# Keys of a linear-attention block transposed by DMA, block steps reordered, and 27 expert tiles turned by TensorE

## The chip, the cores and the metric

The kernel runs on one core of a Trainium2 chip. Its engines are TensorE (PE in the profile, with its weight loads as PEld), VectorE (DVE), ScalarE (ACT), GpSimd (POOL) and SyncE (SP, which here issues DMAs); 16 DMA engines move data for all queues. The metric is the device time of one execution in microseconds, as the median of several runs.

## The reference

The input is x of 8 sequences x 1024 tokens x 256 values, all float32. It is normalised per token, and the result is x plus a linear attention plus a mixture of experts, both of the normalised x.

```python
xn = _layernorm(x)
q = elu(xn @ Wq.T) + 1          # 16 heads of 16
k = elu(xn @ Wk.T) + 1
v = xn @ Wv.T
kv_cumsum = cumsum(einsum('blhd,blhe->blhde', k, v), axis=1)
k_cumsum = cumsum(k, axis=1)
out = einsum('blhd,blhde->blhe', q, kv_cumsum)
out = out / clip(einsum('blhd,blhd->blh', q, k_cumsum), 1e-6)
attention = out @ Wo.T

top, which = top_k(xn @ Wr + br, 2)      # 8 experts
c = softmax(top), put at the two experts
moe = sum over e of c[e] * ((silu(xn @ W1[e]) * (xn @ W3[e])) @ W2[e])   # inner size 512
result = x + attention + moe
```

## The kernel before

**Blocks and tiles.** The 8192 tokens are 16 blocks of 512 (`NBLK`, `TB`), each of four chunks of 128; two blocks make a sequence. The expert work is cut into tiles of 128 (token, expert) pairs, gathered by token number: 25 tiles of the first four blocks (`N1`), and then 107 of all that is left (`NM` = 132 in all; three more run only if the counts need them). A first part, in a `tc.manual_schedule` context, normalises and transposes the first four blocks, computes their router logits, the first lists of tokens, and block 0's q, k and v.

**The main loop.** `for j in range(NM + 1)` makes one pass for each expert tile. For j from 1 to 11 a pass also normalises, turns and routes one more block of x (block 4 + j); these blocks are read into five buffers (`f_x`, tag "xb") by `load_x`, some on SP's queue ahead of the loop, the others on ScalarE's queue five blocks ahead. For j from 12 to 21 a pass also builds a piece of the second lists (`second_batch`, almost all of it on VectorE). Then `attend_upto` makes one or more steps of attention, and `ffn_step(j)` does the expert tile: it gathers tile j + 4 on GpSimd (`ffn_load`), asks for the weights of tile j + 2 on SP (`ffn_weights`), runs the gate and up matmuls of tile j (`ffn_hidden`, L1261, 32 matmuls into two `gu_ps` banks of the four-bank pool `ps_mm`), prepares the transposed input of tile j + 1, and runs the output matmuls of tile j - 1 (`ffn_out`, L1280). Results are added to DRAM by GpSimd (L1291).

**How a tile is transposed.** The matmuls need a tile with its features on the partitions. For j below `TURNED` = 8, `ffn_turn` does it: two TensorE transpositions (L1226) and a ScalarE copy (L1228). Later tiles go as two-byte halves: `ffn_halves` splits each float32 into its low and high 16 bits on VectorE (L1198), `ffn_turn_halves` issues one transposing DMA on SP between the tile's two weight loads (L1207), and `ffn_join` puts the halves together on ScalarE (L1216).

**Steps of a block.** `block_steps(t)` drives the generator `project(t)`, then `scores` and `weigh` for the four chunks; it yields nine times, and each stretch between yields is a step. Of `project`, the pieces were grouped so: step 0 both halves of q (L795; `elu1` on ScalarE and VectorE, `mask_q` on ScalarE) and the output projection (`attend`, L993) of the last block's last chunk; step 1 the keys `kn` (L811); step 2 eight TensorE transpositions of `kn` (L858), the copies to `kT` (L861) and on VectorE the running sum of keys and its product with q (L863 to L868); step 3 the values (L811, copies L828) and the denominators (`den`, L880), whose reciprocals go through DRAM and come back spread over partitions as `rden`. Step 4 asks for the next block's input and makes the first scores (L917, masked by L924 on VectorE, four banks of `ps_mm`). `attend_upto(n)` makes at most n steps in all, at least one a pass if any is due, and joins a step to the one before it in the same pass only if it is step 0, 4 or 8. From pass 22 on, 121 steps are spread over 106 passes.

**What sets the order.** In the `manual_schedule` context the written order holds on TensorE, VectorE, ScalarE and GpSimd. Elsewhere a planner of the language orders each engine's instructions by their place in the program, by when it expects their inputs, and by free buffers; only instructions under `in_order` (all DMAs on SP, the norm and the join on ScalarE) keep the order they are written in. So SP is one strict queue, and a DMA that waits there holds up all later ones.

Of the kernel before, what the change touches and what calls it, by code (L numbers as in the profile page):

```python
# [46 lines left out]
F32 = mybir.dt.float32  # L47
I32 = mybir.dt.int32
BF16 = mybir.dt.bfloat16
U16 = mybir.dt.uint16  # L50
AF = mybir.ActivationFunctionType
ALU = mybir.AluOpType
AX = mybir.AxisListType

P = 128
# [9 lines left out]
def tile_attention_moe(  # L65
# [14 lines left out]
    nc = tc.nc  # L80
    B, L, H = x.shape
    E, _, I = w1.shape
    KC = H // P
    IC = I // P
    TB = 512
    NCH = TB // P
    N = B * L
    NBLK = N // TB
    BLK_PER_SEQ = L // TB
# [4 lines left out]
    FB = 4  # L94
# [4 lines left out]
    NM = NF - NR  # L99
# [11 lines left out]
    two = ctx.enter_context(tc.tile_pool(name="two", bufs=2))  # L111
# [4 lines left out]
    ps_t = ctx.enter_context(tc.tile_pool(name="ps_t", bufs=2, space=bass.MemoryType.PSUM))  # L116
# [4 lines left out]
    f_x = ctx.enter_context(tc.tile_pool(name="f_x", bufs=5))  # L121
# [17 lines left out]
    in_order = tc.keep_in_program_order  # L139
# [7 lines left out]
    def load_x(t, queue):  # L147
        xbs[t] = f_x.tile([P, NCH, H], F32, tag="xb", name=f"xb{t}")
        in_order(queue.dma_start(out=xbs[t], in_=xf[t]))
# [15 lines left out]
    for t in range(FB, FB + 2):  # L165
        load_x(t, nc.sync)

    ident = const.tile([P, P], F32, name="ident")
# [5 lines left out]
        out=causal, in_=causal, pattern=[[1, P]], compare_op=ALU.is_ge,  # L174
# [5 lines left out]
        out=before, in_=before, pattern=[[1, P]], compare_op=ALU.is_ge,  # L180
        fill=0.0, base=-1, channel_multiplier=-1,
    )
    ones = const.tile([P, P], F32, name="ones")
# [5 lines left out]
        out=own, in_=own, pattern=[[-HD, HALF]], compare_op=ALU.is_ge,  # L189
# [583 lines left out]
    sums = [None]  # L773
# [10 lines left out]
    def begin(t):  # L784
        names = dict(
            qT=[KC, TB], qm=[KC, 2, TB], kn=[NCH, H], kT=[KC, TB], rden=[NCH, KC, P]
        )
        tiles = {n: one.tile([P, *d], F32, tag=n, name=n) for n, d in names.items()}
        blocks[t] = tiles["qT"], tiles["qm"], tiles["kT"], tiles["kn"], va, tiles["rden"]
# [27 lines left out]
    def project_k(t, c):  # L817
        kn = blocks[t][3]
        z = project_kv(t, c, 0)
        yield from elu1(  # L820
            kn[:, c : c + 2, :].rearrange("p c h -> p (c h)"), z.rearrange("p c h -> p (c h)")
        )

    def project_v(t, c):
# [6 lines left out]
            )  # L831
        yield

    def project(t):


        if t > 0:
            begin(t)
            for o in range(KC):
                for _ in project_q(t, o):  # L840
                    pass
                mask_q(t, o)
                yield
            for c in range(0, NCH, 2):
                for _ in project_k(t, c):
                    pass
                yield
        else:
            for _ in range(4):
                yield  # L850
        qT, qm, kT, kn, va, rden = blocks[t]
        upto_t = two.tile([P, KC], F32, tag="upto_t", name="upto_t")
        fresh = t % BLK_PER_SEQ == 0
        qks = []
        for o in range(KC):
            tp = ps_t.tile([P, TB], F32, tag="t", name="tp")
            for c in range(NCH):
                nc.tensor.transpose(  # L858
                    tp[:, bass.ts(c, P)], kn[:, c, bass.ts(o, P)], ident
                )  # L860
            nc.scalar.copy(kT[:, o, :], tp)  # L861
            ksum = two.tile([P, TB], F32, tag="ksum", name="ksum")
            nc.vector.tensor_tensor_scan(  # L863
                ksum, ones[:, 0:1].to_broadcast([P, TB]), kT[:, o, :],
                0.0 if fresh else sums[0][:, o : o + 1], ALU.mult, ALU.add,
            )
            nc.vector.tensor_copy(upto_t[:, o : o + 1], ksum[:, TB - 1 : TB])
            nc.vector.tensor_tensor(ksum, qT[:, o, :], ksum, ALU.mult)  # L868
            qks.append(ksum)
            yield  # L870
        for c in range(0, NCH, 2):
            if t > 0:
                for _ in project_v(t, c):
                    pass
            yield

        den = ps_y.tile([P, P], F32, tag="y", name="den")
        for o in range(KC):
            for c in range(NCH):
                nc.tensor.matmul(  # L880
                    den[32 * c : 32 * c + 32, :], lhsT=own_of[:, o, :],
                    rhs=qks[o][:, bass.ts(c, P)], start=(o == 0), stop=(o == KC - 1),
                    skip_group_check=True,
                )
        over = one.tile([P, P], F32, tag="over", name="over")
        nc.vector.tensor_scalar(over, den, EPS_DEN, None, ALU.max)
        nc.vector.reciprocal(over, over)

        through = den_d[t % 2]
        for c in range(NCH):  # L890
            in_order(
                nc.sync.dma_start(
                    out=through[HEADS * c : HEADS * (c + 1)],
                    in_=over[32 * c : 32 * c + HEADS, :].unsqueeze(1).to_broadcast([HEADS, HD, P]),
                )
            )
        in_order(
            nc.sync.dma_start(
                out=rden.rearrange("p c o l -> p (c o) l"),
                in_=through.rearrange("(x h) d l -> (h d) x l", h=HALF),  # L900
            )
        )
        yield
        del xnTs[t]
        sums[0] = upto_t
# [103 lines left out]
    def block_steps(t):  # L1009


        for i, _ in enumerate(project(t)):
            if i == 1 and behind:
                attend(*behind.pop())
            if i in (1, 3, 5, 8):
                yield
        if t + 1 < NBLK:
            fetch(t + 1)
        waiting = scores(t, 0)
        yield  # L1020
        done = None
        for c in range(NCH):
            coming = scores(t, c + 1) if c + 1 < NCH else None
            if done and c + 1 < NCH:
                attend(*done)
            oT = weigh(*waiting)
            if done and c + 1 == NCH:
                attend(*done)
            done = t, c, oT
            waiting = coming  # L1030
            if c + 1 < NCH or t + 1 < NBLK:
                yield
        behind.append(done)
        if t + 1 == NBLK:
            attend(*behind.pop())
            yield
# [97 lines left out]
    with tc.issue_after(last_store[0].ins):  # L1134
        for a in range(4):
            some = slice(a * E // 4, (a + 1) * E // 4)
            in_order(
                nc.sync.dma_start(
                    out=w2_sb.rearrange("p (c h) -> p c h", h=H)[
                        :, a * E * IC // 4 : (a + 1) * E * IC // 4, :  # L1140
                    ],
                    in_=w2[some].rearrange("e (c p) h -> p (e c) h", p=P),
                )
            )
        load_x(FB + 2, nc.sync)

        for t in range(FB):
            rows = slice(t * TB, (t + 1) * TB)
            in_order(nc.sync.dma_start(out=acc_d[rows, :], in_=x_rows[rows, :]))
        in_order(nc.sync.dma_start(out=wo_sb, in_=woT.rearrange("(k p) o -> p k o", p=P)))  # L1150
    table = nc.sync.dma_start(
        out=tab_d[0].rearrange("(p j i) w -> p j (i w)", j=2, i=FT),
        in_=tab.rearrange("p (j i) w -> p j (i w)", j=2)[:, :, 0 : FT * 3],
# [19 lines left out]
    def ffn_load(j):  # L1173
        table, _, num_i, src_i, _, _, i = of_tile(j)
        xg[j] = ffn4.tile([P, H], F32, tag="xg", name="xg")
        nc.gpsimd.indirect_dma_start(  # L1176
            out=xg[j], out_offset=None, in_=x_rows[:, :],
            in_offset=bass.IndirectOffsetOnAxis(ap=src_i[:, i : i + 1], axis=0),
        )
        entry[j] = ffn8.tile([P, 3], F32, tag="entry", name="entry")  # L1180
        nc.gpsimd.indirect_dma_start(  # L1181
            out=entry[j], out_offset=None, in_=table[:, :],
            in_offset=bass.IndirectOffsetOnAxis(ap=num_i[:, i : i + 1], axis=0),
        )
# [114 lines left out]
    def ffn_step(j, behind):  # L1299


        if j + 4 < NM:
            ffn_load(j + 4)
        if j + 2 < NM:
            ffn_weights(j + 2)
        if j < NM:
            ffn_hidden(j, j == NM - 1)
        if j + 1 < TURNED:
            ffn_turn(j + 1)
        elif j + 1 < NM:  # L1310
            ffn_join(j + 1)
        if j > 0 and j != NM - 1:
            ffn_out(j - 1)
        for _ in range(2):
            if stored[0] < j - behind:
                ffn_store(stored[0])
                stored[0] += 1


    TURNED = 8  # L1320
    for j in range(4):
        ffn_load(j)
    for j in range(2):
        ffn_weights(j)
    for i in range(3, 6):
        load_x(FB + i, nc.sync)
    ffn_norm(0)
    ffn_turn(0)
    LATE = 3
# [105 lines left out]
```

## Time and profile before

| | |
|---|---|
| median of 3 runs | 1288.55 us (1285.26 to 1289.98) |
| the profiled execution's own time | 1289.82 us |
| its span, first to last instruction | 1287.7 us |
| mean granted TensorE clock | 0.985 |
| TensorE busy | 1221.5 us |
| VectorE, ScalarE, GpSimd busy | 681.8, 558.6, 522.7 us |
| DMA engines, mean over 300 to 1260 us | 0.87 busy |

Rows of a group are to be read as: line, engine, operation, output<-input, shapes, count, then busy time in us and mean length of one in ns, then the idle time of the engine ahead of them and what ended it. A row of a timeline has start, length, line, engine, what, count, and in brackets a wait ahead of it with its releaser. Lengths of neighbouring matmuls overlap, so the distance from one start to the next tells what one costs in a stream. "SPq" and "ACTq" rows are DMA issues.

### The profile page before, as it was taken

To read this page: it belongs to the slowest core of one execution; us is meant where nothing else is said; L and a number is where in the kernel's file an instruction comes from. 1 tells how busy PE (TensorE), PEld (TensorE's weight loads), DVE (VectorE), ACT (ScalarE), POOL (GpSimd) and SP (SyncE) were. 2 spreads that over 40 slices of the span, in tenths; PEclk is the share of its full clock that TensorE was granted. 3 is DMA by queue.
4 is the path that set the end of the run, shared out by engine and by line. 5 is a ranking of instruction groups with operands and counts; after the bars stand their busy time and mean duration, and the time that the engine had idled before them with its cause. 6 is when DMAs were issued, how large, how long until landed. Compare 5 with 4: busy or idle time off the path is not lost. (4 is left out here: it accounts for less than half of the span.)

```text
span 1287.7 us, 30871 instructions
## 1 busy us (share of the span) xinstructions
PE 1221.5 (95%) x12064; PEld 1046.7 (81%) x12064; DVE 681.8 (53%) x1560; ACT 558.6 (43%) x1060; POOL 522.7 (41%) x460
## 2 busy tenths in 40 slices
PE   5789999899999999999999999999999999999995
PEld 3578786678888888888888888888888888888885
DVE  7867489764354454535453544445453536354541
ACT  4556465372442626262625344262626262444420
POOL 3634334214334444444342534443443534343522
PEclk9889999899999999999999999999999999999998
DMA  9898776659699898889796989989888979897983
GB/s 341 269 293 240 174 196 156 198 136 246 132 277 211 169 222 189 198 188 225 158 234 145 210 182 212 197 173 226 177 206 173 231 168 220 172 211 164 213 186 62
DMA packets 230929, 256.79 MB, mean 199 GB/s; under 512 B 83554, under 2 KB 154850, under 8 KB 230498
## 3 DMA queue, kind: packets, MB, share of 16 engines
q1 hardware_dynamic: 187394, 200.58, 55.6%
q0 software_dynamic: 38064, 43.22, 24.8%
q10 hardware_dynamic: 5328, 11.01, 2.4%
q8 instruction: 99, 1.62, 0.6%
q14 instruction: 44, 0.36, 0.1%
HBM read 196.30 MB, written 52.67 MB: 193 GB/s over the span
## 5 line engine op out<-in xcount | busy, mean ns | idle before, releaser
L1261 PE MATMUL gu_ps<-xgT,w 128*128 128x128 f32 x4224 | 514.0, 279 | 19.5 <-DVE s_sb L924 8.3
L1261 PEld LDWEIGHTS gu_ps<-xgT,w 128*128 128x128 f32 x4224 | 493.6, 194 | 37.3 <-DVE s_sb L924 12.2
L1291 POOL DMA_INDIRECT out_dram<-y,dst_i x107 | 175.8, 1643 | 296.3 <-issue 67.2
L1280 PE MATMUL y_ps<-w_sb,hT 128*128 x1056 | 251.2, 380 | 1.5 <-DVE hT L1272 0.9
L1176 POOL DMA_INDIRECT xg<-in_x_dram,src_i x132 | 130.6, 990 | 244.4 <-DVE half L1198 183.7
L1269 ACT ACTIVATE hT<-gu_ps 128x512 f32<-128x512 f32 x132 | 78.8, 597 | 321.2 <-PE gu_ps L1261 320.9
L1280 PEld LDWEIGHTS y_ps<-w_sb,hT 128*128 128x128 f32 x1056 | 190.4, 190 | 23.6 <-DVE hT L1272 1.0
L924 DVE TENSOR_TENSOR s_sb<-s_ps,causal 128x512 f32<-128x512 f32 x256 | 162.8, 683 | 70.5 <-PE o_ps L951 41.3
L1198 DVE COPY half<-xg 128x512 uint16<-128x512 uint16 x124 | 54.3, 438 | 149.1 <-ACT xg L1188 148.9
L1272 DVE TENSOR_TENSOR hT<-gu_ps,hT 128x512 f32<-128x512 f32 x132 | 90.5, 685 | 65.9 <-PE gu_ps L1261 42.2
L1181 POOL DMA_INDIRECT entry<-tab_d,of_i x107 | 106.1, 992 | 36.6 <-issue 32.0
L1287 DVE TENSOR_SCALAR y<-y_ps,entry 128x256 f32<-128x256 f32 x132 | 63.6, 482 | 107.3 <-PE y_ps L1280 107.0
L998 ACT COPY at<-a_ps 128x256 f32<-128x256 f32 x64 | 23.6, 370 | 168.0 <-PE a_ps L993 168.0
L1216 ACT COPY xgT<-halfT 128x512 uint16<-128x512 uint16 x124 | 94.1, 759 | 5.4 <-DMA halfT<-half 5.4
L917 PE MATMUL s_ps<-qm,kT 32*128 32x256 f32 x1024 | 86.5, 406 | 2.0 <-DVE hT L1272 1.9
L1291 POOL DMA_INDIRECT acc_d<-y,src_i x25 | 41.7, 1669 | 99.7 <-DVE y L1287 46.8
L1188 ACT ACTIVATE xg<-xg,entry 128x256 f32<-128x256 f32 x132 | 78.4, 594 | 3.9 <-DMA xg<-in_x_dram,src_i 3.2
L917 PEld LDWEIGHTS s_ps<-qm,kT 32*128 32x128 f32 x1024 | 51.6, 184 | 26.3 <-issue 19.4
L993 PE MATMUL a_ps<-wo_sb,oT 128*128 128x256 f32 x256 | 71.6, 403 | 1.0 <-DVE oT L968 1.0
L951 PE MATMUL o_ps<-s_sb,va 128*32 128x128 f32 x2048 | 69.5, 274 | 0.0
L993 PEld LDWEIGHTS a_ps<-wo_sb,oT 128*128 128x128 f32 x256 | 45.8, 194 | 23.1 <-issue 14.4
L795 PE MATMUL zq<-xnT,wq_sb 128*128 128x512 f32 x128 | 60.2, 610 | 0.0
(213 smaller groups left out, 1316.3 us busy)
## 6 DMA issues: line engine op xcount, KB each, us to landing
w<-in_w_dram SPq DMA_DIRECT2D x264, 512.0 KB
den_d<-over SPq DMA_DIRECT2D x64, 128.0 KB
rden<-den_d SPq DMA_DIRECT2D x16, 512.0 KB
xnT_d<-xnT ACTq DMA_DIRECT2D x15, 512.0 KB
xnT<-xnT_d SPq DMA_DIRECT2D x15, 512.0 KB
out_dram<-in_x_dram SPq DMA_DIRECT2D x12, 512.0 KB
out_dram<-at POOLq DMA_DIRECT2D x12, 512.0 KB
xb<-in_x_dram SPq DMA_DIRECT2D x10, 512.0 KB
```

Source lines behind the costliest of these rows:

```text
L917: nc.tensor.matmul(s_ps[r][:, hh].rearrange("p a l -> p (a l)"), lhsT=kT[rows, hh, span], rhs=qm[rows, hh, :, span], start=True, stop=True,)
L924: nc.vector.tensor_tensor(sm, s_ps[r].rearrange("p k a l -> p (k a) l"), causal_b, ALU.mult)
L993: nc.tensor.matmul(a_ps, lhsT=oT[:, hh, :], rhs=wo_sb[:, hh, :], start=(hh == 0), stop=(hh == 1),)
L1176: nc.gpsimd.indirect_dma_start(out=xg[j], out_offset=None, in_=x_rows[:, :], in_offset=bass.IndirectOffsetOnAxis(ap=src_i[:, i : i + 1], a ...
L1181: nc.gpsimd.indirect_dma_start(out=entry[j], out_offset=None, in_=table[:, :], in_offset=bass.IndirectOffsetOnAxis(ap=num_i[:, i : i + 1], ...
L1188: nc.scalar.activation(xg[j], xg[j], AF.Identity, bias=entry[j][:, 1:2], scale=entry[j][:, 2:3])
L1216: nc.scalar.copy(xgT[j].bitcast(U16).rearrange("p k (l b) -> p b k l", b=2), halves.pop(j).rearrange("p (b k) l -> p b k l", b=2),)
L1261: done = nc.tensor.matmul(ps[:, i, :], lhsT=w13[:, k, bass.ts(i, P)], rhs=xgT[j][:, k, :], start=(k == 0), stop=(k == KC - 1),)
L1269: silu = nc.scalar.activation(hT, gu[0], AF.Silu)
L1272: nc.vector.tensor_tensor(hT, gu[1], hT, ALU.mult)
L1280: done = nc.tensor.matmul(y_ps, lhsT=hT[:, i, :], rhs=w2_sb[:, bass.ds(e * (IC * H) + i * H, H)], start=(i == 0), stop=(i == IC - 1),)
L1291: nc.gpsimd.indirect_dma_start(out=rows[:, :], out_offset=bass.IndirectOffsetOnAxis(ap=dst_i[:, i : i + 1], axis=0), in_=ys.pop(j), in_off ...
```

## The change

The keys of blocks 1 to 15 are no longer transposed by TensorE. In `project`, step 0 now makes the keys and splits them on VectorE into two planes of 16-bit halves (`planes`, in buffers of the pool that held x). Step 1 issues four transposing DMAs on SP and makes q. Step 2 makes the values, joins the transposed halves on ScalarE into `kT`, and runs the key sums. Step 3 has the denominators alone. The held-back `attend` follows the first piece. Block 0 keeps TensorE transpositions. x of blocks 7 and 8 is asked for on SP ahead of the store of the table, block 9's after the first weights. `TURNED` is 27, and until pass 22 a tile is gathered three passes ahead, then four as before.

```diff
+    def key_sums(t, o, upto_t, qks):
+        qT, kT = blocks[t][0], blocks[t][2]
+        ksum = two.tile([P, TB], F32, tag="ksum", name="ksum")
+        nc.vector.tensor_tensor_scan(
+            ksum, ones[:, 0:1].to_broadcast([P, TB]), kT[:, o, :],
+            0.0 if t % BLK_PER_SEQ == 0 else sums[0][:, o : o + 1], ALU.mult, ALU.add,
+        )
+        nc.vector.tensor_copy(upto_t[:, o : o + 1], ksum[:, TB - 1 : TB])
+        nc.vector.tensor_tensor(ksum, qT[:, o, :], ksum, ALU.mult)
+        qks.append(ksum)
+
+    def planes(name):
+        tile_ = f_x.tile([P, NCH, H], F32, tag="xb", name=name)
+        return tile_.rearrange("p c h -> p (c h)").bitcast(U16)
+
     def project(t):
+        upto_t = two.tile([P, KC], F32, tag="upto_t", name="upto_t")
+        qks = []
         if t > 0:
             begin(t)
+            kT, kn = blocks[t][2:4]
+            halves_k = planes("k_half").rearrange("p (c b h) -> p c b h", c=NCH, b=2)
+            for c in range(0, NCH, 2):
+                for _ in project_k(t, c):
+                    pass
+                nc.vector.tensor_copy(
+                    halves_k[:, c : c + 2],
+                    kn[:, c : c + 2].bitcast(U16).rearrange("p c (h b) -> p c b h", b=2),
+                )
+            yield
+            turned_k = planes("k_halfT").rearrange("p (b o l) -> p b o l", b=2, o=KC)
+            for c in range(NCH):
+                in_order(
+                    nc.sync.dma_start_transpose(
+                        out=turned_k.rearrange("p b o l -> p (b o) l")[:, :, bass.ts(c, P)],
+                        in_=halves_k[:, c].rearrange("p b h -> p (b h)"),
+                    )
+                )
             for o in range(KC):
                 for _ in project_q(t, o):
                     pass
                 mask_q(t, o)
-                yield
+            yield
             for c in range(0, NCH, 2):
-                for _ in project_k(t, c):
-                    pass
-                yield
...
                 for _ in project_v(t, c):
                     pass
+            for o in range(KC):
+                nc.scalar.copy(
+                    kT[:, o].bitcast(U16).rearrange("p (l b) -> p b l", b=2),
+                    turned_k[:, :, o],
+                )
+                key_sums(t, o, upto_t, qks)
             yield
...
         for i, _ in enumerate(project(t)):
-            if i == 1 and behind:
+            if i == 0 and behind:
                 attend(*behind.pop())
-            if i in (1, 3, 5, 8):
-                yield
+            yield
...
         in_order(nc.sync.dma_start(out=wo_sb, in_=woT.rearrange("(k p) o -> p k o", p=P)))
+        for t in range(FB + 3, FB + 5):
+            load_x(t, nc.sync)
...
-        if j + 4 < NM:
-            ffn_load(j + 4)
+        while loaded[0] < min(NM, j + (5 if j >= READ else 4)):
+            ffn_load(loaded[0])
+            loaded[0] += 1
...
-    TURNED = 8
-    for j in range(4):
+    TURNED = 27
+    for j in range(3):
         ffn_load(j)
+    loaded = [3]
     for j in range(2):
         ffn_weights(j)
-    for i in range(3, 6):
-        load_x(FB + i, nc.sync)
+    load_x(FB + 5, nc.sync)
```

Block 0's branch does what the old code did for every block (eight transpositions, copies, key sums), with the sums moved into `key_sums`.

More of the change, by code (lines that the diff above doesn't have):

```diff
@@ L842, in project @@
                 mask_q(t, o)
-                yield
+            yield
             for c in range(0, NCH, 2):
-                for _ in project_k(t, c):
-                    pass
-                yield
-        else:
-            for _ in range(4):
-                yield
[L851 to L872, printed above, removed]
                 for _ in project_v(t, c):
                     pass
-            yield
+            for o in range(KC):
[4 more added lines that the diff above has]
+                key_sums(t, o, upto_t, qks)
+            yield
+        else:
+            kT, kn = blocks[t][2:4]
+            yield
+            yield
+            for o in range(KC):
+                tp = ps_t.tile([P, TB], F32, tag="t", name="tp")
+                for c in range(NCH):
+                    nc.tensor.transpose(
+                        tp[:, bass.ts(c, P)], kn[:, c, bass.ts(o, P)], ident
+                    )
+                nc.scalar.copy(kT[:, o, :], tp)
+                key_sums(t, o, upto_t, qks)
+            yield
+        rden = blocks[t][5]
         den = ps_y.tile([P, P], F32, tag="y", name="den")
@@ L1012, in block_steps @@
         for i, _ in enumerate(project(t)):
-            if i == 1 and behind:
+            if i == 0 and behind:
                 attend(*behind.pop())
-            if i in (1, 3, 5, 8):
-                yield
+            yield
         if t + 1 < NBLK:
```

## The prediction, made before the changed kernel ran

> **What bounds the kernel now.** I read the page first: the busy times, then the span in 40 slices.
>
> ```profile
> PE 1221.5 (95%) x12064; PEld 1046.7 (81%) x12064; DVE 681.8 (53%) x1560; ACT 558.6 (43%) x1060; POOL 522.7 (41%) x460
> ...
> PE   5789999899999999999999999999999999999995
> ```
>
> TensorE is the bound from about the sixth slice on, and no other engine is near it. Over 300 to 1260 us it is busy 947 of 960 us, and its waits there come to 12.5 us, 5.3 of them (8 waits, 0.7 at most) for the mask multiplication L924. So whatever leaves TensorE in that stage is worth its full price, and work on the other engines costs nothing unless TensorE comes to wait for it. The timeline of TensorE in one block (start, length, line, what) shows the price list:
>
> ```profile
> 566.05 3.62 PE L811 MATMUL zkk<-wkv_sb,xnT 128*128 128x256 f32 x16
> 569.50 3.73 PE L1261 MATMUL gu_ps<-xgT,w 128*128 128x128 f32 x32
> 573.07 1.89 PE L1280 MATMUL y_ps<-w_sb,hT 128*128 x8
> 574.80 1.04 PE L858 MATMUL tp<-ident,kn 128*128 128x128 f32 x8
> 575.67 3.74 PE L1261 MATMUL gu_ps<-xgT,w 128*128 128x128 f32 x32
> 579.25 1.89 PE L1280 MATMUL y_ps<-w_sb,hT 128*128 x8
> 580.98 3.62 PE L811 MATMUL zkv<-wkv_sb,xnT 128*128 128x256 f32 x16
> 584.52 0.64 PE L880 MATMUL den<-ksum,own_of 128*32 128x128 f32 x16
> 585.10 1.36 PE L917 MATMUL s_ps<-qm,kT 32*128 32x256 f32 x16
> 587.11 3.84 PE L1261 MATMUL gu_ps<-xgT,w 128*128 128x128 f32 x32 [0.66 <-DVE s_sb L924]
> ```
>
> Each row starts where the last one's stream ends, so a row costs the distance to the next start. The eight transpositions of the keys cost 575.67 - 574.80 = 0.87 us, and one wait of 0.66 us stands after den and scores.
>
> Then the first 100 us, in windows (us, busy us of PE, PEld, DVE, ACT, POOL, clock, DMA share, GB/s):
>
> ```profile
> 36.00:40.00 4.00, 2.60 (x21) 1.81 (x25) 3.90 (x9) 3.94 (x12) 3.59 (x4) 1.00 0.55 203
> 40.00:44.00 4.00, 3.15 (x62) 2.27 (x61) 1.78 (x8) 1.64 (x5) 0.18 (x1) 1.00 0.31 84
> 44.00:48.00 4.00, 3.88 (x18) 2.19 (x16) 4.00 (x17) 3.98 (x8) 3.09 (x4) 1.00 1.04 347
> 48.00:52.00 4.00, 0.00 (x0) 0.00 (x0) 3.48 (x21) 0.80 (x3) 3.09 (x4) 0.82 1.04 352
> ```
>
> The DMA engines idle at 36 to 44 and are full from 44, while TensorE stands still at 48 to 52: ScalarE waits until 51.5 for the first gathered tile (issued 45.4), the first expert's input.
>
> **The change, part by part.**
>
> *Keys off TensorE.* Blocks 1 to 15 lose eight transpositions each: 15 x 0.87 = **-13.0 us**. Here a rule has to be weighed. The row has 273 ns for one:
>
> ```profile
> L858 PE MATMUL tp<-ident,kn 128*128 128x128 f32 x128 | 17.4, 273 | 0.0
> L1226 PE MATMUL xg_t<-ident,xg 128*128 128x128 f32 x16 | 3.5, 294 | 4.3 <-ACT xg L1188 4.3
> L1198 DVE COPY half<-xg 128x512 uint16<-128x512 uint16 x124 | 54.3, 438 | 149.1 <-ACT xg L1188 148.9
> L1216 ACT COPY xgT<-halfT 128x512 uint16<-128x512 uint16 x124 | 94.1, 759 | 5.4 <-DMA halfT<-half 5.4
> L861 ACT COPY kT<-tp 128x512 f32<-128x512 f32 x32 | 17.3, 587 | 9.2 <-PE tp L858 9.0
> ```
>
> The Trainium skill (TensorE: Matmul & The Clock Gate, Part 4, PE-mode transpose) puts one at about 275 ns in a kernel, mostly access latency. The row's length agrees, but in a stream these latencies overlap: 109 ns from start to start. By the page's figure this part would be -33 us and the next +10; I take the starts.
>
> *Tiles 8 to 26 turned by TensorE.* 19 tiles x 2 transpositions: at 118.02 such a pair stands in the stream and the next row starts at 118.24, so 19 x 0.22 = **+4.2 us** (+3.5 with the five tiles that fall into the stage where VectorE is the limit free, +5.6 at 294 ns each). ScalarE copies 0.37 us in place of 0.76, VectorE loses 19 copies of 0.43, SP 19 issues of 1.21 us. At 220 to 240 us VectorE is busy 19.15 of 20 us and TensorE only 14.94, with one wait of 4.2 us for a joined tile (xgT, L1216). Tiles of passes 12 to 21 are in this stretch: some eight copies, 3.5 us, go from VectorE, but the halves of blocks 1 and 2 bring 3.2 back. What is left is the shorter chain of a tile: between 0 and -4.2, taken as **-1**.
>
> *x read ahead.* 1 MB (two loads of 512 KB) moves from behind the first weights (SP, 44.2 us) to ahead of the table store, into the idle stretch. At 350 GB/s it takes 3.0 us out of the full stretch. Two waits can shrink: the first tile's at 48 to 52, and VectorE's 5.0 us at 75.8 to 80.8 for a later x load, after which TensorE waits 1.5 and 3.0 us (L917, L1261). The table is issued at 36.8 and first read at 43.8, so 3 us in front of it are covered; uncovered they would cost 3. Between +3 and -6, taken as **-3**, the bytes' own time once. Gathers are issued one tile later until pass 22, two passes ahead of use (15 us) against 6 us of landing: nothing.
>
> *What is added to a block, all beside TensorE.* VectorE: two copies of 128x1024 halves, between 0.7 (start to start of the 512 form, doubled) and 0.88 us each. In the keys' step they fit between the two kn results and hT, which waits for ScalarE's table load and SiLU until 7.6 us after the step begins anyway. Such copies run 512 elements in 0.43 us, and the skill (SBUF - State Buffer, the "DVE blocks DMA" trap) warns that a fast VectorE copy shuts GpSimd out while it writes descriptors. By the rule that is up to 30 x 0.88 = 26 us of GpSimd time; it is busy 41%, and its longest wait, 183.7 us for half (L1198), is for a buffer that is gathered two passes early. No TensorE wait, so 0. ScalarE: two joins of 128x1024 take the place of two kT copies (L861), 1.16 to 1.52 us against 0.59; step 2 then holds 4 va copies (1.3 us), joins (2.7), SiLU, join and norm of a tile (1.9): 5.9 of 9.2 us.
>
> SP: four transposing issues of 1.21 us (5 us), in order ahead of that pass's weights. They wait for the halves, done 7.5 us after the keys' step begins; behind them w1 of tile X+2 goes out at about 11.5 instead of 7.3 us, the tile's own transposition and w3 follow, and ScalarE and TensorE want those at 23 us and later. They land 3.3 us after issue (547.57 to 550.9), the last at 14.5 us; the joins' step begins at 18.4. **0**, with 4 us of cover for the joins. The DMA engines: the packet records show 512 packets of 256 B for each transposition, 24.5 ns each, 0.78 us of all 16 engines. 60 come and 19 go: +32 us over a span with 0.87 busy; no weight is waited for now.
>
> *Order of the steps.* Keys and q change places: both take 3.5 us of TensorE. But v now carries the key sums (scan, product: 3.7 us of VectorE), and den comes right after, where before the cheap transposition step lay a pass earlier. If ScalarE joins before it copies v, the sums end 5 us into the pass, before hT, and nothing is late. If after, joins end at 6.9 us, the sums at 9.4, hT at 10.0, y at 10.4: den waits 0.3, scores 0.2, the next gu_ps 1.45 instead of 0.66 us. Ten of the 15 blocks have den and scores in one pass. Between 0 and +13; the written order is not binding outside the first section and ScalarE is idle 3.5 us ahead of v (L828), so I take **+1.3**.
>
> Sum: -13.0 + 4.2 - 1 - 3 + 1.3 = **-11.5 us**. The profiled execution took 1289.8 us (span 1287.7 and 2.1 around it), 1.3 above the median of 1288.55. It would become 1278.3, the median **1277.0**.
>
> **Rivals.** (B) *Den and scores come late.* VectorE has the sums behind the joins in ten blocks: the upper value above, 13 instead of 1.3: 1288.7. For it: L924 is already the largest wait; against: the idle ScalarE. (C) *Slower: the joins wait for their transposition in ScalarE's strict order.* If the order places joins as soon as data is expected (pass of q) and four transpositions land later than that, SiLU, xgT and so gu_ps queue behind. At 2 us in each of 15 blocks: 1277.0 + 30 = 1307. It decides from 1.2 us a block (18 us turn -11.5 into +6.5). For it: the DMA engines show shares over 1.0 in many windows; against: 124 transpositions today cost ScalarE two waits, 5.4 us in all. (D) *The first 300 us give more:* both early waits (4.5 us) and the 4.2 us wait at 240 go, 5 more than taken: 1272.
>
> **How the numbers follow.** This case 0.50 (1272 to 1283 by the bounds of its terms), D 0.17, B 0.20, C 0.13. About 0.5%, 6.4 us, is what a measurement of this kernel can tell: faster is below 1282.1, slower above 1295. Faster: 0.46 + 0.17 + a tail of B, 0.64; same: 0.04 + 0.17 of B, 0.21; slower: C and 0.02 of B, 0.15. The range, 1268 to 1291, leaves out C and the end of D.
>
> **What would show it.** L858 at x8 only; xg_t (L1226) at x54 and 0.22 us a pair; the order keys, q, v, den on TensorE with no row of 0.87 us between; no wait of den L880 over 0.3 us and L924 still about 5 to 7 us over 300 to 1260 (B: 15 and more); ScalarE's waits for the transposed keys near zero (C: 30 and more); TensorE starting gu_ps before 53.3 us. The prediction is wrong if the stretch from tile 23 to the end isn't some 11 us shorter, whatever the first 300 us do.

## The result, and the profile after

The changed kernel takes 1377.78 us (median, 1372.89 to 1382.55) against 1288.78 for the kernel before, measured beside it: ratio 1.0684, 95% interval 1.0656 to 1.0711. It is 6.8% slower where -0.9% was forecast, and far outside the range of 1268 to 1291.

The profiled execution has a span of 1380.8 us at a granted clock of 0.958 (before: 1287.7 at 0.985). The page's first lines, as they were read before:

```profile
PE 1240.4 (90%) x11982; PEld 1056.2 (76%) x11982; DVE 702.9 (51%) x1571; ACT 603.9 (44%) x1086; POOL 519.7 (38%) x460
...
PE   5789998989699998989898999989898999979796
```

TensorE has 82 matmuls fewer and is nevertheless busy 19 us longer, and the slices from the ninth on are no longer solid nines. The chain of waits names the place; a row has the engine and line that waited, the releaser, the sum in us, how many times, the longest.

```profile
DVE ksum L838 <- ACT kT L885: 130.3, 27, 16.1
ACT kT L885 <- DMA k_halfT<-k_half: 122.0, 13, 13.0
...
PE zkv L811 <- DVE qT L765: 71.4, 13, 10.7
```

ScalarE's joins (L885) wait 122.0 us for the transposed keys, 13 times. VectorE's key sums wait for the joins. And TensorE's projection of the values waits 71.4 us, also 13 times, for half of q (`qT`). Before, it had no wait at all:

```profile
L811 PE MATMUL zkv<-wkv_sb,xnT 128*128 128x256 f32 x256 | 58.1, 379 | 0.0
```

What have the values to do with q? The tenth block, number 9 when counted from 0 as below, shows it. ScalarE from the end of the keys' pass:

```profile
814.91 0.60 ACT L1218 ACTIVATE xg<-xg,entry 128x256 f32<-128x256 f32 x1
824.86 1.33 ACT L885 COPY kT<-k_halfT 128x1024 uint16<-128x1024 uint16 x1 [9.35 <-DMA k_halfT<-k_half]
826.07 0.58 ACT L762 ACTIVATE neg<-zq 128x512 f32<-128x512 f32 x1
826.55 1.32 ACT L885 COPY kT<-k_halfT 128x1024 uint16<-128x1024 uint16 x1
827.88 1.28 ACT L763 ACT_TABLE_LOAD   x1
829.18 0.63 ACT L763 ACTIVATE neg<-neg 128x512 f32<-128x512 f32 x1
```

The first join stands *ahead* of q's activations (L762, L763) on ScalarE, though it is written a step behind them. It waits 9.35 us, and q waits behind it. TensorE in the same block:

```profile
806.75 3.62 PE L811 MATMUL zkk<-wkv_sb,xnT 128*128 128x256 f32 x16
...
816.36 3.60 PE L795 MATMUL zq<-xnT,wq_sb 128*128 128x512 f32 x8
819.80 3.73 PE L1291 MATMUL gu_ps<-xgT,w 128*128 128x128 f32 x32
823.37 1.89 PE L1310 MATMUL y_ps<-w_sb,hT 128*128 x8
830.59 5.21 PE L811 MATMUL zkv<-wkv_sb,xnT 128*128 128x256 f32 x16 [5.33 <-DVE qT L765]
836.07 3.84 PE L1291 MATMUL gu_ps<-xgT,w 128*128 128x128 f32 x32 [0.27 <-ACT xgT L1246]
```

q's two sums (`zq`) and the tile's two `gu_ps` hold all four banks of `ps_mm`. They are read out by q's activations, so the values can't start until 830.59: a wait of 5.33 us. And the row itself is 5.21 us long instead of 3.62. Windows over the last wait and the row (columns as in the prediction, the clock being the third number from the end):

```profile
824.00:830.50 6.50, 1.26 (x6) 0.76 (x4) 3.54 (x5) 5.59 (x7) 0.38 (x1) 0.98 0.88 278
830.50:836.00 5.50, 5.21 (x16) 4.04 (x16) 2.41 (x5) 5.46 (x8) 2.10 (x2) 0.71 0.08 7
```

After a standstill of 5.3 us the granted clock is 0.71; in block 6, after 4.6 us, it is 0.50. The Trainium skill (TensorE: Matmul & The Clock Gate, Part 1) has a rule for this: an idle window of about 3.4 us throttles the array to half its clock, and about 3.4 us of activity release it. From the page's figures one would estimate that a standstill costs 1.7 us more than its length. Measured over blocks 3 to 15, the sixteen matmuls of the values take 77.0 us in place of 13 x 3.62 = 47.1: 30.0 us, or 2.3 a block (0.1 to 3.1), which is more than that estimate. Nor is the edge sharp here: behind a standstill of 3.12 us (block 13) they take 3.72 us, behind one of 3.20 (block 4) 5.24.

The two sums, 71.4 + 30.0 = **101.4 us**, can be set against a ruler: the start of the output matmuls (`y_ps`) of tile 24, and of the last tile, 131, in each kernel. Blocks 3 to 15 lie between.

```
us                               to tile 24   24 to 131
before                              337.5       935.1
changed                             337.5      1030.1
changed, joins unfed                329.6       927.5
```

So up to tile 24 nothing was won or lost by the whole change, and behind it 1030.1 - 927.5 = 102.6 us hang on what the joins wait for. The last row is the first experiment, in which the joins read data that need no DMA ("unfed").

### The profile page after: what moved, and what is told of

Read it like the earlier page. It is cut to its first block, busy times and chain, and to the rows that moved or that the text cites. A ratio compares the mean times of both kernels' runs of the same rounds, so it can differ in the third digit from the quotient of the medians.

```text
span 1380.8 us, 30847 instructions
## 1 busy us (share of the span) xinstructions
PE 1240.4 (90%) x11982; PEld 1056.2 (76%) x11982; DVE 702.9 (51%) x1571; ACT 603.9 (44%) x1086; POOL 519.7 (38%) x460
## 5 line engine op out<-in xcount | busy, mean ns | idle before, releaser
L1321 POOL DMA_INDIRECT out_dram<-y,dst_i x107 | 172.4, 1611 | 306.4 <-DVE y L1317 176.5
L811 PE MATMUL zkv<-wkv_sb,xnT 128*128 128x256 f32 x256 | 90.3, 524 | 71.4 <-DVE qT L765 71.4
L811 PEld LDWEIGHTS zkv<-wkv_sb,xnT 128*128 128x128 f32 x256 | 67.8, 274 | 91.3 <-DVE qT L765 76.6
L1228 DVE COPY half<-xg 128x512 uint16<-128x512 uint16 x105 | 45.0, 429 | 131.3 <-ACT xg L1218 131.2
L885 ACT COPY kT<-k_halfT 128x1024 uint16<-128x1024 uint16 x30 | 39.6, 1329 | 122.0 <-DMA k_halfT<-k_half 122.0
L1246 ACT COPY xgT<-halfT 128x512 uint16<-128x512 uint16 x105 | 79.5, 757 | 0.2 <-DMA halfT<-half 0.2
L946 PEld LDWEIGHTS s_ps<-qm,kT 32*128 32x128 f32 x1024 | 50.1, 185 | 26.2 <-issue 20.6
```

The source lines that it names most:

```text
L811: nc.tensor.matmul(z[:, i, :], lhsT=xnTs[t][:, k, bass.ts(c + i, P)], rhs=wkv_sb[:, k, a, :], start=(k == 0), stop=(k == KC - 1),)
L946: nc.tensor.matmul(s_ps[r][:, hh].rearrange("p a l -> p (a l)"), lhsT=kT[rows, hh, span], rhs=qm[rows, hh, :, span], start=True, stop=True,)
L1246: nc.scalar.copy(xgT[j].bitcast(U16).rearrange("p k (l b) -> p b k l", b=2), halves.pop(j).rearrange("p (b k) l -> p b k l", b=2),)
L1321: nc.gpsimd.indirect_dma_start(out=rows[:, :], out_offset=bass.IndirectOffsetOnAxis(ap=dst_i[:, i : i + 1], axis=0), in_=ys.pop(j), in_off ...
```

## The experiments

**Theory W**, formed on this trace: the loss is one thing, the wait of two instructions that stand too early in ScalarE's strict order; the transpositions cost nothing by themselves. Against it stands **L**: the 60 transpositions load SP's queue and the DMA engines, and weights or tiles come late, with the waits as a symptom. And **O**: the new order of the steps is what costs. A third question is the second half of the change (x ahead, 27 tiles).

### Joins that wait for nothing

The joins read the halves as they are, not transposed; the transpositions are issued and nobody reads them. The output is that of other keys.

```diff
-                    kT[:, o].bitcast(U16).rearrange("p (l b) -> p b l", b=2),
-                    turned_k[:, :, o],
+                    kT[:, o].bitcast(U16).rearrange("p (c h b) -> p b c h", c=2, b=2),
+                    halves_k[:, 2 * o : 2 * o + 2].rearrange("p c b h -> p b c h"),
```

> The changed kernel, but the joins read the halves as they were before the transposition, from VectorE's own copy; so what lies in kT is not the transposed keys, and the outputs are those of other keys. The 60 transposing DMAs are still issued, unread. Only the wait of the joins for a DMA is taken away, at an early place on ScalarE. Theory W: 1275 to 1290 us, TensorE waits for qT under 5 us. Theory L: the DMAs run as before, 1360 to 1380 us. Theory O: 1350 to 1380 us.

Measured: 1270.83 us, ratio 0.9864 (0.9844 to 0.9884), 4 us below the range expected. All 60 transpositions are there, and the values' matmuls wait for nothing:

```profile
L811 PE MATMUL zkv<-wkv_sb,xnT 128*128 128x256 f32 x256 | 60.5, 387 | 0.0
```

L falls, and with it O, since the steps have the new order. Not only the wait is gone, though: the planner now puts the first join still earlier, 6.0 us behind the keys' step in block 9 where it was free for it at 8.8, so the key sums come early too.

```profile
758.80 1.35 ACT L885 COPY kT<-k_half 128x1024 uint16<-128x1024 uint16 x1 [0.21 <-DVE k_half L863]
```

Two copies ahead of q therefore cost nothing by themselves; they cost when they stand there and wait. This kernel, 17 us faster than before, shows what the change could give if the data were there in time.

### The order alone, and the second half alone

```diff
-                nc.scalar.copy(
-                    kT[:, o].bitcast(U16).rearrange("p (l b) -> p b l", b=2),
-                    turned_k[:, :, o],
-                )
+                tp = ps_t.tile([P, TB], F32, tag="t", name="tp")
+                for c in range(NCH):
+                    nc.tensor.transpose(
+                        tp[:, bass.ts(c, P)], kn[:, c, bass.ts(o, P)], ident
+                    )
+                nc.scalar.copy(kT[:, o, :], tp)
```

The changed kernel with the keys turned by TensorE in the values' step, no halves and no transposing DMAs for them:

> The changed kernel with the keys of every block transposed by TensorE in the values' step (eight transpositions and the two kT copies), no halves and no transposing DMAs for keys; the order keys, q, v, den, the earlier x and the 27 turned tiles stay. Theory W: without a DMA to wait for, about 13 us above what the changed kernel would have without its wait: 1286 to 1300 us. Theory L: the same. Theory O: the order itself costs, 1350 us and more.

Measured: 1284.37 us, 0.9958 (0.9931 to 0.9986), 2 below the range expected. The kernel before with x ahead, 27 tiles turned and the gathers changed:

> The kernel before with the second part of the change alone: x of blocks 7 and 8 ahead of the table, 27 tiles turned by TensorE, tiles gathered three passes ahead until pass 22; keys and order of steps as before. By the prediction's terms +4.2 for the 38 transpositions, -1 and -3 for the first 300 us: 1286 to 1291 us, about the same as before. If this part had a share in the loss: 1300 us and more. If the rival with the larger gain in the first 300 us was right: 1281 to 1285 us.

Measured: 1282.75 us, 0.9952 (0.9936 to 0.9969), better than the 1286 to 1291 of the prediction's terms. Of its 5.4 us, 5.3 are there at tile 24 (332.2 against 337.5), and the stretch behind is as before (935.3). The traces show where they come from. Before, TensorE waits once for a joined tile at about 240 us, and the clock falls; here that tile is turned by TensorE, and the wait is gone. The wait before, then 235 to 250 us before and in this run:

```profile
PE gu_ps L1261 <- ACT xgT L1216: 4.2, 1, 4.2
235.00:250.00 15.00, 10.82 (x119) 8.97 (x118) 9.92 (x22) 3.78 (x12) 2.53 (x3) 0.77 0.35 95
235.00:250.00 15.00, 13.15 (x146) 10.33 (x145) 12.03 (x28) 5.00 (x20) 4.30 (x4) 1.00 0.40 129
```

The medians of the two kernels of this section differ by 1.6 us, which would be the order's price, but their intervals overlap; the keys off TensorE are the 13.5 us from 1284.37 to 1270.83.

To see whether the x loads have a part in it, the kernel before with these moved alone:

```diff
+        for t in range(FB + 3, FB + 5):
+            load_x(t, nc.sync)
...
-    for i in range(3, 6):
-        load_x(FB + i, nc.sync)
+    load_x(FB + 5, nc.sync)
```

> The kernel before with only the x loads of two blocks moved ahead of the table's store; tiles, gathers and keys as before. By the prediction's term: 1285.6 (3 us less). By the trace of the run with both parts of the second half, where the first gu_ps began 2.2 us later and the table's issue 1.2 us later: 1288 to 1292, and then the 19 more tiles turned by TensorE are worth 5 to 8 us off, not 3.2 us on.

Measured: 1289.18 us, 1.0008 (0.9993 to 1.0023): no difference. Its windows (same columns) and the first tile show why:

```profile
40.00:44.00 4.00, 2.77 (x54) 2.16 (x55) 1.77 (x7) 2.85 (x8) 0.00 (x0) 1.00 0.71 239
44.00:48.00 4.00, 3.94 (x18) 2.26 (x16) 4.00 (x17) 4.00 (x8) 2.52 (x3) 1.00 0.93 301
```

```profile
54.15 0.69 PE L1228 MATMUL xg_t<-ident,xg 128*128 128x128 f32 x2 [6.21 <-ACT xg L1190]
55.30 6.02 PE L1263 MATMUL gu_ps<-xgT,w 128*128 128x128 f32 x32 [0.46 <-ACT xgT L1230]
```

The idle DMA time at 40 to 44 us (share 0.31 before) is used now, but the table's store moved with it (issued at 37.2 instead of 36.8 us), and the first gu_ps begins at 55.3 instead of 53.3 us. What is won later is lost here: tile 24 begins at 338.0. The wait of 4.2 us for a joined tile is still there in this run. So the second half's gain, 5.4 + 0.3, comes from the tiles that TensorE turns, together with the gathers issued one pass later; no run parts these two.

### The joins held behind the step ahead of them

```diff
-                nc.scalar.copy(
+                in_order(nc.scalar.copy(
                     kT[:, o].bitcast(U16).rearrange("p (l b) -> p b l", b=2),
                     turned_k[:, :, o],
-                )
+                ))
```

`in_order` forbids the planner to pull a join ahead of ScalarE's earlier bound instructions.

> The changed kernel with one difference: the two joins of the keys keep their written place among ScalarE's ordered instructions, so they stand behind the SiLU of q's pass and behind the copies of v, no longer ahead of q's activations. Every DMA, copy and transposition stays. Theory W (the joins wait on ScalarE for transpositions that land some 18 us after the keys' step begins, and hold up q, its PSUM banks and so the values' matmuls): the joins now start about 22 us after the keys' step, so their wait of 122 us falls under 15, TensorE's 71 us wait for qT (L765) vanishes, and the time is 1277 to 1290 us. Theory L (the 60 added transpositions load the DMA engines and SP's queue, which makes everything later): nothing of that has changed, 1360 to 1380 us. Theory O (the order keys, q, v, den with key sums beside the values costs it): 1360 to 1380 us as well, and the waits for L953 and L909 are 30 us and more.

Measured: 1303.23 us, 1.0129 (1.0102 to 1.0156): 75 us of the loss are gone with nothing changed in the program but the place of two instructions of a block. It is still above the 1277 to 1290 that W gave. The joins stand behind the four copies of the values now and wait for nothing (2.6 us in block 3), and the next thing is late: the sums of keys, and the denominators behind them.

```profile
PE den L909 <- DVE ksum L843: 21.3, 16, 2.4
```

That is 1.3 us a block; the stretch from tile 24 takes 948.6 us.

### The joins first in the values' pass

The joins and the sums are written ahead of the values' projection, and bound as above: two joins, four copies, SiLU.

```diff
+            for o in range(KC):
+                in_order(nc.scalar.copy(
+                    kT[:, o].bitcast(U16).rearrange("p (l b) -> p b l", b=2),
+                    turned_k[:, :, o],
+                ))
+                key_sums(t, o, upto_t, qks)
             for c in range(0, NCH, 2):
                 for _ in project_v(t, c):
                     pass
-            for o in range(KC):
-                nc.scalar.copy(
...
-                key_sums(t, o, upto_t, qks)
             yield
```

> The changed kernel complete, but in a block's second step the joins and the key sums are written ahead of the values' projection and the joins are kept in that order on ScalarE: two joins, then four copies of v, then SiLU. The joins so stand at the start of the values' pass, about 18.4 us after the keys' step begins; the four transpositions landed 18.2 us after it in the changed kernel's trace. Theory W (the loss is the wait of ScalarE's joins, put where the data isn't there yet): no wait for k_halfT over 1 us a block, sums done before den, so neither the 122 us of joins waiting nor the 21 us of den waiting remain: 1271 to 1280, below the kernel before. If the sums are still late for den: about 1.3 us a block, 1290 to 1303. Theory L (the loss is the load of the transpositions on DMA and SP): 1370 or more.

Measured: 1281.65 us, 0.995 (0.9933 to 0.9967), 2 above the range expected, and on this chip faster than both kernels. ScalarE in the tenth block, whose keys' step begins at 761.61:

```profile
776.74 2.54 ACT L805 ACTIVATE qm<-qT,par 128x512 f32<-128x512 f32 x4
...
782.20 2.53 ACT L882 COPY kT<-k_halfT 128x1024 uint16<-128x1024 uint16 x2
784.60 1.18 ACT L828 COPY va<-zkv 128x256 f32<-128x256 f32 x4
```

The joins begin 20.6 us behind the keys' step, without a wait (3.2 us in block 3). From tile 24 on it takes 928.4 us, 1 more than with unfed joins. But it is at tile 24 only at 337.4. There blocks 1 and 2 lie, in the stretch where VectorE builds the lists, and the joins of block 2 stand 12 us behind the values.

### Twice the transpositions

```diff
-            for c in range(NCH):
+            for c in (*range(NCH), *range(NCH)):
```

> The changed kernel with each of a block's four transposing DMAs issued twice, eight in a row instead of four; the joins wait for all eight. With the later data the planned order puts the joins between the copies of v instead of ahead of q's activations. Theory W: though SP and DMA do double the work for the keys and the data land some 25 us after the keys' step instead of 18, the time falls, since the joins no longer stand ahead of q: 1300 to 1335 (sums late for den by 2 to 4 us a block). Theory L: the doubled load adds about as much again as the change lost: 1430 or more.

Measured: 1319.6 us, 1.0229 (1.0206 to 1.0253). With eight transpositions a block the kernel is 58 us *faster* than with four. The planner, which goes by when it expects the data, puts the joins between the copies of the values instead of ahead of q:

```profile
807.43 0.63 ACT L828 COPY va<-zkv 128x256 f32<-128x256 f32 x2
809.81 2.56 ACT L885 COPY kT<-k_halfT 128x1024 uint16<-128x1024 uint16 x2 [1.74 <-DMA k_halfT<-k_half]
```

They still wait, but 28.5 us in all and with q already done. This is the clearest sign against L: the data land later here than in the changed kernel, and the kernel is faster, since less stands behind the waiting instruction.

### The first half without the second

TURNED 8, x and gathers as before, the rest as changed.

> The changed kernel without its second half: x of blocks 7 and 8 loaded where it was before, gathers as before, 8 tiles turned by TensorE as before. Theory W: the joins still stand ahead of q's activations and wait some 9 us for the transposed keys in 13 blocks, so 1375 to 1390; the second half of the change is worth some 5 us either way and takes no part in the loss. If the loss came from the two halves meeting (x ahead and the other gathers shifting the plan): below 1320.

Measured: 1399.25 us, 1.0855 (1.082 to 1.0889), 9 above the upper end expected. The wait is the same (123.7 us of joins, 13 times; tile 24 to 131 takes 1032.2), so the loss doesn't need the second half. But the second half is worth more here than 5: tile 24 begins at 347.0 instead of 337.5. The wait for a joined tile is back in this trace (4.5 us at 225 to 260 us); that the rest comes from the halves of the keys and of the tiles meeting on VectorE in the list stage was only argued.

### Blocks 1 and 2 as before

Blocks 1 and 2 in the old order with TensorE's transpositions, 3 to 15 with the joins first.

```diff
+        if t in (1, 2):
+            begin(t)
...
+            for o in range(KC):
+                tp = ps_t.tile([P, TB], F32, tag="t", name="tp")
+                for c in range(NCH):
+                    nc.tensor.transpose(
+                        tp[:, bass.ts(c, P)], kn[:, c, bass.ts(o, P)], ident
+                    )
+                nc.scalar.copy(kT[:, o, :], tp)
+                key_sums(t, o, upto_t, qks)
+            yield
+            for c in range(0, NCH, 2):
+                for _ in project_v(t, c):
+                    pass
-        if t > 0:
+        elif t > 0:
```

> The kernel with the joins first, but blocks 1 and 2, whose keys fall into the list stage, in the order and way of before (q, keys, transposition of the keys by TensorE with the sums, values, denominators); blocks 3 to 15 by DMA with the joins ahead of v. If what parts the joins-first kernel from the one with unfed joins lies in these two blocks (tile 24 began y_ps at 337.4 against 329.6 us, at 332.2 with TensorE's keys in the old order; from tile 24 to the last 928.5 and 927.5): tile 24 at about 332, the rest 928.5, so 1274 to 1279. If it isn't the placement of these two blocks' keys and sums: 1281 to 1284, and tile 24 at 336 or later.

This run fell on another chip, on which the kernel before takes 1314.47 us. Measured: 1316.16, ratio 1.001 (0.9986 to 1.0034). It missed the 1274 to 1279 expected, and by itself answers nothing about the two blocks. So it was put beside the joins-first kernel:

> The kernel with blocks 1 and 2 in the old order on TensorE and 3 to 15 by DMA with the joins first, once more beside the joins-first kernel itself on one chip, since the last run fell on a chip where the kernel before takes 1314 us. By tile 24's start and the later pace in the earlier traces: 5 us below the joins-first kernel, tile 24 at about 332 on a chip of 1289 us. If these two blocks aren't where it loses: no difference.

> The joins-first kernel, unchanged, as the partner of the mixed one: 0.995 of the kernel before on a chip of 1289 us, as before. On a chip of 1314 us[...], nearer 1.0.

On the chip of 1314 us again: 1314.02 (1.0016, 0.9986 to 1.0046) and 1322.22 (1.0054, 1.0027 to 1.008). The mixed kernel is 8 us below its partner, where 5 was expected (the two intervals just overlap), and tile 24 begins 10 us earlier (336.1 against 346.4). But neither beats the kernel before there. To tell whether on such a chip the transpositions aren't free after all, three kernels went together:

> The changed kernel whose joins read halves that were never turned (the output is that of other keys; the 60 transpositions are issued, and nothing waits for them), once more, beside two others on one chip. On a chip where the kernel before takes about 1289 us: 0.986 again. On one where it takes 1314 us: also 0.985 to 0.990 if that chip only loses time to something that all kernels share, 1.00 if there the 60 transpositions themselves, read by nobody, hold up other transfers (theory L).

> Keys turned by TensorE in the values' step, new order, x ahead and 27 tiles turned: no transposition of keys by DMA. 0.996 where the kernel before takes 1289 us. Where it takes 1314 us: 0.996 again if the order of the steps isn't what costs more there; above 1.003 if it is.

> Blocks 1 and 2 in the old order on TensorE, blocks 3 to 15 by DMA with joins first. Where the kernel before takes 1289 us: 0.988 to 0.992, by tile 24's start and the later pace of the two traces named with the first run of it. Where it takes 1314 us: 1.00 again, and the order kernel beside it tells whether that is the order (it too at 1.00 or more) or the transposition by DMA (it at 0.996).

They fell on a chip of 1289.93 us: 1272.57 (0.9876, 0.9838 to 0.9915), 1283.19 (0.995, 0.9931 to 0.9969), and the mixed kernel at **1278.24 us, 0.9898 (0.9865 to 0.9932)**, the best ratio of a complete one. The ruler shows both halves of it:

```
us                               to tile 24   24 to 131
joins first                         337.4       928.4
blocks 1 and 2 as before            332.0       928.6
joins unfed, second time            329.7       926.3
keys by TensorE, second time        334.8       932.8
```

What the chip of 1314 us takes away stays open. The trace of the joins-first kernel shows there

```profile
PE gu_ps L1291 <- issue: 21.4, 13, 4.5
```

against 11.3 us on the other chip, waits for which the profile names no releaser. Slower DMA packets are not it: those of 2 KB take 105 ns on both chips. No trace of the kernel before is kept from there, and the new order with the keys turned by TensorE was not run there, so neither the transpositions nor the order can be ruled out.

## Why the prediction was wrong

**The step that failed** is the one on SP: "They land 3.3 us after issue (547.57 to 550.9), the last at 14.5 us; the joins' step begins at 18.4. **0**, with 4 us of cover for the joins." Two things in it were wrong, and the second turned the first into a loss.

*The landing.* The joins were released 3.6 us later than predicted. SP in the tenth block:

```profile
813.48 6.67 SPq L871 DMA_TRANSPOSE k_halfT<-k_half  x4
820.72 0.37 SPq L1272 DMA_DIRECT2D w<-in_w_dram  x1
```

The issues take 1.67 us each, not 1.21, but they also begin earlier, 6.7 us behind the keys' step instead of 7.5, so the last one goes out at 11.2, as in the prediction (11.1). What was mis-sized is the time from there: the first join is released at 18.1, 6.9 us behind the start of the last issue, not 3.3. The 3.3 was a misreading. In the trace of before, the packets of that very transposition (issued at 547.57) run from 550.3 to 551.6, and the semaphore updates that tell of its landing end at 552.7, after 5.1 us; the median of all such landings at 300 to 1230 us is 5.9 us. So a row of four costs little beyond four issues; a single one was already slower than taken. Of the 4 us of cover, 0.3 were left in the tenth block, and in six of the 13 blocks the release came later than 18.4 (it ranges from 15.9 to 24.3).

*The place.* The joins did not stand in their step. The planner put them where it expected the data, which was ahead of q: ScalarE was free for them at 815.5 (824.86 - 9.35), 8.8 us behind the keys' step. Even a landing at 14.5 us would have left 5.7 us of waiting. The prediction had the rule itself ("the written order is not binding outside the first section"), but its main case used it only for joins ahead of the values' copies, not for joins ahead of q.

The two errors multiply. With the joins in a later place nearly nothing is lost although the landing is just as late (joins first), so the place is what turns the landing into a loss. But the size comes from the landing: in blocks 4 to 15 TensorE's wait is the release less 12.8 us, so a release at 14.5 would have left about 1.7 us a block, some 22 us in place of 71.4, an estimate from these rows that no run has tried. The run with doubled transpositions shows that a better place can outweigh a later landing.

**Rival C had the mechanism**, with its place: "If the order places joins as soon as data is expected (pass of q) and four transpositions land later than that". Its size was off: 2 us a block were put, and it is 102.6 / 13 = 7.9. What stood behind the join was not SiLU first but q's activations, which free the PSUM banks that the values need, and each standstill then slowed the clock: 5.5 us of waiting and 2.3 of slower matmuls. The argument against C, 5.4 us of waits for 124 transpositions of tiles, was no evidence: a tile's join is bound to its written place, and the joins of the keys were not.

**Rival B** came true only with the joins behind the values' copies. There the denominators wait 1.3 us a block, and the stretch takes 948.6 - 928.4 = 20.2 us longer than with the joins first, more than B's 11.7.

**The other terms.** *Keys off TensorE*, -13.0: 13.5 us by one pair of runs and 10.6 by the other, right; the -33 of the latency that the prediction set aside is far from both. *The stretch from tile 23*, "some 11 us shorter": from tile 24 on the unfed kernel is 7.5 to 8.7 us shorter than the kernel before, the joins-first one 6.6. But block 3, at the edge of the list stage, lies between tiles 24 and 28 and goes otherwise. Counted from tile 28, with twelve blocks to come at 0.87 us (10.4 us):

```
us                               tile 28 to 131
before                              892.8
the second half alone               892.9
the order alone                     892.9
joins unfed, both times             883.7, 882.6
joins first                         882.5
```

There the keys' price comes out (9.1 to 10.3 us), and the order costs nothing. *Order*, +1.3 for late denominators: 1.6 us by the first pair of medians and about 0 by the second run of it (0.995 against 0.9952), so not clear of noise; and the term's reason doesn't hold, since what the order costs, if anything, is lost ahead of tile 28. That it came out near is luck. *Tiles turned and list stage*, +4.2 - 1: wrong in sign, about -5.7. The prediction named the wait of 4.2 us for a joined tile at 240 us, but took it as -1 and left the rest to rival D; the whole wait went, and with it the slow clock that followed. *x ahead*, -3: about 0 (-0.9 to +3.0). The first tile came 2 us later, against the sign that was expected of it ("gu_ps before 53.3 us"). *Copies on VectorE beside GpSimd*, 0: a gather of a tile takes 0.97 us of GpSimd with unfed joins and 0.98 before, so nothing of that shows.

**Signs named ahead.** Transpositions of keys by TensorE x8 and of tiles x54: both as said. No row of 0.87 us between keys, q, v and den: so. Waits of den and of the mask multiplication (B: 15 and more): 0.2 us and none at 300 to 1230 us, so B did not come. ScalarE's waits for the transposed keys "near zero (C: 30 and more)": 122. That sign tells C from the rest.

## What to carry to other kernels

When an instruction moves to another engine's strict queue and gets its data from a DMA, ask where in that queue the scheduler will put it and what stands behind it, not when its written step begins: here two copies of 1.3 us in each of 13 blocks, placed some 9 us ahead of their data, cost 103 us through PSUM banks that q's activations had to free. Bind such an instruction to the latest place from which its consumer is still served, and take a DMA's landing from the event that releases its reader, over many of them. Where the bound engine stands still behind a chain of other engines, moving the chain's work onto it can be a gain, not a price.

## What the runs showed that was not expected

A standstill of TensorE of 3 to 11 us is paid for again by slower work: the 16 matmuls behind it take 5.2 to 6.7 us instead of 3.62 in 12 of 13 blocks (3.72 in the other). Doubling the DMAs made the changed kernel 58 us faster, through the place that the planner gave to their reader. And the joins-first kernel's gain of 0.5% on one chip was a loss of 0.5% on another, where the kernel before takes 2% longer: a small verdict from one chip is worth repeating on a second.
